# GpSimd's tiles as a subtraction and a max with zero, in halves, in place of eight pointer-scalar minima

## The chip, the cores and the metric

The kernel runs on one core of a Trainium2 chip. A core has TensorE (PE in the profile), VectorE (DVE), ScalarE (ACT), GpSimd (POOL) and SyncE (SP), which here only issues DMAs. Each engine works through its own instruction stream in order; semaphores order the engines against each other. The metric is device time of one launch in microseconds, as the median of several runs. All data are float32.

## The reference, cut to what matters

Four graph layers run over 64 graphs of 256 nodes with 128 features. Each takes `relu(layernorm(x))` and adds its result to x. Layers 0 to 2 are matrix products with a 256 x 256 adjacency and small weights, with gates, and together they make the "front" of the kernel below. Layer 3 is the heavy one: it needs, for every pair of nodes (i, j) of a graph and each of 256 hidden features, one leaky ReLU.

```
def _L3_gnn_ref(x, W, b_lin, a, bias):          # W and bias are the adjacency
    W1, W2 = (W[:, :F], W[:, F:])
    s1 = jnp.einsum('bkf,ef->bke', x, W1)
    s2 = jnp.einsum('bkf,ef->bke', x, W2)
    pre = s1[:, :, None, :] + s2[:, None, :, :] + b_lin
    h = jnp.where(pre >= 0, pre, ALPHA * pre)
    e = jnp.einsum('bije,e->bij', h, a) + bias
    attn = jax.nn.softmax(e, axis=2)
    out = jax.nn.sigmoid(jnp.einsum('bij,bjf->bif', attn, x))
```

A leaky ReLU is ALPHA times its argument plus (1 - ALPHA) times the ReLU. The part linear in s1 drops out of the softmax, the part linear in s2 is one product (`lin`), and what is left is the sum over e of a[e] (1 - ALPHA) relu(s1[i, e] + s2[j, e]).

## The kernel before

Graphs are handled in 32 pairs (NB = 2). For one pair, `front(p)` computes layers 0 to 2 and the operands of layer 3: s1 in two feature halves, `s1a` (features 0 to 127) and `s1b` (128 to 255), each 128 partitions x 2 graphs x 256 nodes, and minus s2 in the same two halves. The first half of minus s2 stays in a PSUM bank (`s2a`) with a copy in SBUF (`s2c`); the second is in SBUF (`s2n`), and ScalarE copies it to a PSUM bank (`s2p`) for itself.

The work of layer 3 is cut into tiles `rl` of 128 features x 4 rows i x 2 graphs x 256 nodes j, that is 128 x 2048 float32. A pair needs 128 tiles: 2 blocks of 128 rows (`ic`), 32 tiles to a block, 2 feature halves. The whole kernel makes 4096. Three engines make them, `work_on_tile(e)`, line 637:

- VectorE makes tiles of the first half alone, each as one minimum of two repeated operands (line 652): min(s1, -s2).
- ScalarE makes tiles of either half with eight activations relu(s1 - (-s2)), 128 x 256 each (line 665). It takes a tile of the first half only where that half lags by two tiles (`half`, line 624).
- GpSimd makes tiles of the second half with eight minima, 128 x 256 each, of `s2n` with a per-partition scalar that is read from a column of `s1b` (line 672). They are made in four parts of two instructions.

min(s1, -s2) is s1 minus relu(s1 + s2), and what is constant over j drops out of the softmax; so a tile of minima serves as well as one of ReLUs, with the weight's sign turned. TensorE sums a tile over the features (`score`, line 696): for each of 4 rows one matmul with a window of weights, `win` for tiles of ReLUs and `win_n` (the negative) for tiles of minima. Two records stand in the trace for each such float32 matmul, so a tile leaves eight.

When a block's 64 tiles are scored, `tail` (line 554) adds the adjacency on VectorE, `lin` on GpSimd (line 562), then softmax and the product with h3, and ends on GpSimd (lines 601 and 602) with the output. GpSimd also takes part in each layernorm (`inverse_root`, lines 258 and 259, and line 331).

The order is not left to the hardware. While the program is built, a planner (lines 751 to 785) plays the schedule with a clock for each engine and a booked cost for each step (`ran`), and `in_order` ties every engine's instructions to the order that came out. What the planner books for tiles is: 2.2 us for a tile of VectorE; 1.43 us (second half, from PSUM) or 1.6 us (first half, from SBUF) for four activations, half a tile; 1.8 us for two minima of GpSimd, a quarter of a tile. Steps of tails go ahead of steps of fronts, and these ahead of tiles; TensorE scores the tile that was done first. There are 13 tile buffers, and an engine holds at most 8 (VectorE), 3 (ScalarE) or 2 (GpSimd) tiles that are being made or wait to be scored. Which engine makes which tile, and when TensorE scores it, is thus fixed by the booked costs; at run time an engine that is later than planned makes TensorE wait at that place in its order. Fronts run about two pairs ahead; a front is spread over 1.7 pairs' worth of scored tiles.

```
    tiles = [[relu_pool.tile([P, 4, NB, N], F32, name=f"rl{k}", bufs=1), 0.0] for k in range(13)]
    MOST = {DVE: 8, ACT: 3, POOL: 2}
```

Of the kernel before, what the change touches and what calls it, by code (L numbers as in the profile page):

```python
# [10 lines left out]
OP = mybir.AluOpType  # L11
# [3 lines left out]
P = 128  # L15
NB = 2
# [4 lines left out]
PE, DVE, ACT, POOL = ENGINES = (mybir.EngineType.PE, mybir.EngineType.DVE, mybir.EngineType.Activation, mybir.EngineType.Pool)  # L21
# [4 lines left out]
def kernel(  # L26
# [19 lines left out]
    a_vec: bass.AP,  # L46
    out: bass.AP,
):

# [25 lines left out]
    nc = tc.nc  # L77
    B, N, D = x.shape
# [19 lines left out]
    def ran(engine, us, *after):  # L98
        start = max(clock[engine], 0.0, *after)
        if engine == ACT:  # L100
            behind[0] = max(0.0, behind[0] - (start - clock[ACT])) + 0.024 * us
        clock[engine] = start + us
        return clock[engine] + SEEN[engine] + (behind[0] if engine == ACT else 0.0)
# [19 lines left out]
    last, done = {}, [0]  # L123
# [112 lines left out]
    win = const.tile([P, NE, 63], F32, name="win")  # L236
    nc.vector.memset(win, 0.0)
    win_n = const.tile([P, NE, 63], F32, name="win_n")
# [27 lines left out]
    def flat(t):  # L266
        return t.rearrange("p b n -> p (b n)")
# [353 lines left out]
    def where(n):  # L621
        return n // SLOTS, n % SLOTS // 32, n % 32

    def half(e):

        return 0 if e == DVE or e == ACT and following[0] <= following[1] - LAG else 1

    def tile_ready(e):

        if e in begun:  # L630
            return 0.0
        n = following[half(e)]
        if n >= NSLOT or n // SLOTS not in READY or held[e] == MOST[e] or not tiles:
            return None
        return max(READY[n // SLOTS]["since"][half(e)], min(t[1] for t in tiles))

    def work_on_tile(e):
        if e not in begun:
            k = half(e)
            tiles.sort(key=lambda t: t[1])  # L640
            begun[e] = [following[k], k, *tiles.pop(0), 0]
            following[k] += 1
            held[e] += 1
        n, k, t, free, part = begun[e]
        p, ic, r = where(n)
        ops = READY[p]
        i0 = ic * P + r
        since = max(ops["since"][k], free)
        if e == DVE:
            whole = [P, 4, NB, N]  # L650
            rows = ops["s1"][0][:, :, i0:i0 + 97:32].rearrange("p b g -> p g b").unsqueeze(3)
            nc.vector.tensor_tensor(t, rows.to_broadcast(whole), ops["s2a"].unsqueeze(1).to_broadcast(whole), op=OP.min)  # L652
            done = ran(DVE, 2.2, since)
            t_s2v[p % 2] = done
            parts = 1
        elif e == ACT:
            if k and "s2p" not in ops:
                ops["s2p"] = s2p
                nc.scalar.copy(s2p, ops["s2n"])
                ran(ACT, COPY, since)  # L660
            parts = 2
            for g in (2 * part, 2 * part + 1):
                for b in range(NB):
                    i = i0 + g * 32
                    nc.scalar.activation(t[:, g, b, :], (s2p if k else ops["s2c"])[:, b, :], AF.Relu,  # L665
                                         bias=ops["s1"][k][:, b, i:i + 1], scale=-1.0)
            done = ran(ACT, 1.43 if k else 1.6, since)
        else:
            parts = 4
            for b in range(NB):  # L670
                i = i0 + part * 32
                nc.gpsimd.tensor_scalar(t[:, part, b, :], ops["s2n"][:, b, :], ops["s1"][1][:, b, i:i + 1], None, op0=OP.min)  # L672
            done = ran(POOL, 1.8, since)
        begun[e][4] += 1
        if part + 1 == parts:
            del begun[e]
            made.append((done, n, k, t, e))
# [18 lines left out]
    def score(tile_):  # L696
        since, n, k, t, e = tile_
        p, ic, r = where(n)
        block = p * NC + ic
        pe = pes[block % 2]  # L700
        first = block not in left
        if first:
            left[block] = 64
        made.remove(tile_)
        left[block] -= 1

        w = win if e == ACT else win_n
        for g in range(4):
            nc.tensor.matmul(pe[g * 32:(g + 1) * 32, :], w[:, k, 31 - r:63 - r], flat(t[:, g]),  # L709
                             start=first, stop=(left[block] == 0), skip_group_check=True)  # L710
        free = ran(PE, PROJECT, since, t_pe.get(block - 2, 0.0))
        tiles.append([t, free])
        held[e] -= 1
        scored[0] += 1
        if left[block] == 0:
            begin((p, ic), tail(p, ic, pe, free, READY[p]["x3"], READY[p]["h3"]))
# [6 lines left out]
    def begin(key, steps):  # L723
        CHAINS[key] = [steps, next(steps), 0]
# [7 lines left out]
    def chain_ready(key, e):  # L732

        engine, since, bank, gate = (*CHAINS[key][1], 0, None)[:4] if len(CHAINS[key][1]) < 4 else CHAINS[key][1]
        if engine != e or bank and not spare or gate and not gate():
            return None
        if not isinstance(key, tuple) and key > 0 and spare:

            due = STEPS_OF_FRONT * (scored[0] / (2 * SLOTS) - (key - 2)) / SPREAD
            if CHAINS[key][2] > due + AHEAD:  # L740
                return None
        return max(since, min(b[1] for b in spare)) if bank else since
# [12 lines left out]
    while scored[0] < 2 * NSLOT or CHAINS:  # L755
        while begun_fronts[0] < NPAIR and begun_fronts[0] < 2 + (scored[0] + 2 * SLOTS - 1) // (2 * SLOTS):
            begin_front()
        e = min(now, key=now.get)
        todo = []
        for key in CHAINS:  # L760
            since = chain_ready(key, e)
# [6 lines left out]
        else:  # L768
            since = tile_ready(e)
# [3 lines left out]
        if ready:  # L773
            _, (rank, *_), what = min(ready, key=lambda x: x[1])
            if rank < 2:
                advance(what)
            elif e == PE:
                score(what)
            else:
                work_on_tile(e)  # L780
            in_order()
            now[e] = max(now[e], clock[e])
        else:
            later = [x[0] for x in todo] + [t for t in now.values() if t > now[e]]
            now[e] = min(later) if later else now[e] + 1.0
# [31 lines left out]
```

## Time and profile before

| | |
|---|---|
| median of 3 runs | 5349.16 us (5348.2 to 5349.51) |
| the profiled execution, its own time | 5354.23 us |
| its span, first to last instruction | 5352.4 us |
| TensorE clock granted | 0.996 |
| tiles by VectorE, ScalarE, GpSimd | 2015, 1415, 666 |
| first minimum of GpSimd starts, last one starts | 140.3 us, 5337.2 us |
| last layernorm step on GpSimd (line 258) | 5122.9 us |

The tile counts come from the groups of instructions: 2015 of line 652; 11320 of line 665 (11056 of the second half and 264 of the first) over eight; 5328 of line 672 over eight. A time in a row "busy" is the union of a group's instructions, so that overlapping ones count once; "mean ns" is the duration of one, and on ScalarE and GpSimd consecutive instructions overlap. All four compute engines are busy for 96 to 98 per cent of the span, so the share of busy time alone does not say which of them sets the pace.

### The profile page before, as it was taken

The page shows a single profiled execution, that of the slowest core. Times are in us where ns is not written, and L with a number is a line of the kernel's source. Part 1 is how long each engine was busy: PE and PEld are TensorE (multiplying, and loading weights), DVE is VectorE, ACT ScalarE, POOL GpSimd, SP SyncE. Part 2 cuts the span into 40 slices and gives each one's busy share as a digit, 9 for nine tenths or more (in the row PEclk, how much of TensorE's full clock was granted, in tenths as well). Part 3 has the DMA queues.
Part 4 walks back from the last instruction along what each step waited for, and adds up shares of the span by engine and source line. Part 5 has one row for each costly group of instructions (what it writes and reads, how often), then busy time and mean ns, then how long its engine had stood idle before and what let it go on. Part 6 is the DMA issues. An engine that isn't in the chain of part 4 may idle for free.

```text
span 5352.4 us, 138977 instructions
## 1 busy us (share of the span) xinstructions
PE 5241.4 (98%) x56085; PEld 1861.5 (35%) x56085; DVE 5221.7 (98%) x4322; ACT 5121.4 (96%) x13465; POOL 5160.9 (96%) x5974
## 2 busy tenths in 40 slices
PE   6999999999999999999999999999999999999998
PEld 2333333333333333333333333333333333333332
DVE  3999999999999999999999999999999999999998
ACT  3999999999999999999999999999999999999999
POOL 0999999999999999999999999999999999999999
PEclk9999999999999999999999999999999999999999
DMA  0000000000000000000000000000000000000000
GB/s 17 5 5 6 6 3 6 6 5 6 5 4 6 5 6 5 3 6 6 5 5 4 4 6 5 6 6 3 6 5 6 6 5 3 6 5 4 4 2 4
DMA packets 38839, 26.99 MB, mean 5 GB/s; under 512 B 3504, under 2 KB 38192, under 8 KB 38192
## 3 DMA queue, kind: packets, MB, share of 16 engines
q1 hardware_dynamic: 35088, 17.05, 1.1%
q8 instruction: 438, 7.18, 0.6%
q14 instruction: 209, 1.71, 0.1%
q10 hardware_dynamic: 3104, 1.05, 0.1%
HBM read 9.70 MB, written 8.39 MB: 3 GB/s over the span
## 4 chain that ended last, share of the span: by engine, by line
PE 49%; DVE 34%; POOL 9%; ACT 5%; issue 4%; DMA 0%; POOLq 0%; SPq 0%; DVEq 0%; ACTq 0%
PE bank L709 32%; DVE rl L652 28%; PE bank L264 15%; POOL rl L672 7%; ACT rl L665 3%; PE bank L292 1%; DVE d L404 1%; DVE stats L324 1%; DVE bank L408 1%; DVE hT L412 1%; DVE rh L385 1%; PE bank L285 1%; POOL sc L562 0%; DVE mv L327 0%; POOL mv L259 0%
## 5 line engine op out<-in xcount | busy, mean ns | idle before, releaser
L672 POOL TENSOR_SCALAR rl<-s2n,s1b 128x256 f32<-128x256 f32 x5328 | 4786.0, 940 | 9.7 <-ACT s1b L539 9.7
L652 DVE TENSOR_TENSOR rl<-s1a,bank 128x2048 f32<-128x2048 f32 x2015 | 4484.6, 2276 | 12.1 <-ACT s1a L548 12.1
L665 ACT ACTIVATE rl<-bank,s1b 128x256 f32<-128x256 f32 x11056 | 4392.2, 839 | 1.3
L709 PE MATMUL bank<-rl,win_n 128*32 128x512 f32 x21448 | 2654.8, 593 | 33.9 <-DVE rl L652 31.9
L709 PE MATMUL bank<-rl,win 128*32 128x512 f32 x11320 | 1487.2, 593 | 0.0
L709 PEld LDWEIGHTS bank<-rl,win_n 128*32 128x32 f32 x21448 | 678.9, 110 | 1496.4 <-issue 1214.0
L709 PEld LDWEIGHTS bank<-rl,win 128*32 128x32 f32 x11320 | 365.9, 110 | 754.4 <-issue 630.2
L264 PE MATMUL bank<-adj_t,h 128*32 128x256 f32 x5120 | 310.0, 381 | 3.8 <-ACT h L423 3.8
L264 PEld LDWEIGHTS bank<-adj_t,h 128*32 128x32 f32 x5120 | 166.6, 110 | 174.3 <-issue 58.6
L335 ACT ACTIVATE h<-x,mv 128x128 f32<-128x128 f32 x384 | 172.1, 634 | 43.3 <-POOL mv L331 42.9
L264 PE MATMUL bank<-hT,u3t 128*32 128x512 f32 x1280 | 169.5, 593 | 0.0
L264 PE MATMUL bank<-mT,w4t 128*32 128x512 f32 x1280 | 169.4, 592 | 0.0
L264 PE MATMUL bank<-mT,w 128*32 128x512 f32 x1280 | 166.8, 593 | 0.5 <-ACT bank L381 0.5
L264 PE MATMUL bank<-mT,w5t 128*32 128x512 f32 x1280 | 166.7, 592 | 0.4 <-DVE rh L385 0.4
L264 PE MATMUL bank<-rh,u5t 128*32 128x512 f32 x1280 | 166.6, 592 | 0.0
L341 ACT COPY mT<-bank 128x512 f32<-128x512 f32 x160 | 133.9, 837 | 33.1 <-PE bank L264 24.6
L396 ACT ACTIVATE bank<-bank,gate_b 128x512 f32<-128x512 f32 x160 | 141.0, 881 | 17.7 <-PE bank L264 17.7
L381 ACT ACTIVATE bank<-bank,gate_b 128x512 f32<-128x512 f32 x160 | 140.0, 875 | 15.6 <-PE bank L264 15.2
L399 ACT ACTIVATE bank<-bank,gate_b 128x512 f32<-128x512 f32 x160 | 136.3, 852 | 12.8 <-PE bank L264 12.8
L423 ACT COPY h<-bank 128x512 f32<-128x512 f32 x128 | 117.3, 916 | 29.6 <-PE bank L292 24.7
L258 POOL TENSOR_SCALAR mv<-mv 128x4 f32<-128x4 f32 x128 | 29.8, 232 | 120.1 <-DVE mv L326 112.5
L404 DVE TENSOR_TENSOR d<-bank,hT 128x512 f32<-128x512 f32 x160 | 108.4, 678 | 37.5 <-ACT bank L399 37.5
(116 smaller groups left out, 3445.0 us busy)
## 6 DMA issues: line engine op xcount, KB each, us to landing
xin<-in_x_dram SPq DMA_DIRECT2D x64, 128.0 KB, 2.3
out_dram<-o SPq DMA_DIRECT2D x64, 128.0 KB, 1.8
w_raw<-in_L_gnn_w_w_dram ACTq DMA_DIRECT2D x3, 128.0 KB, 4.3
th_raw<-in_L_gnn_Theta_dram ACTq DMA_DIRECT2D x1, 320.0 KB, 3.1
adj_n<-in_adj_dram SPq DMA_DIRECT2D x1, 256.0 KB, 4.8
w_raw<-in_L_gnn_u_w_dram ACTq DMA_DIRECT2D x2, 64.0 KB, 3.4
bias<-in_L_gnn_bias_dram ACTq DMA_DIRECT2D x2, 64.0 KB, 3.0
w<-in_L_gnn_weight_dram ACTq DMA_DIRECT2D x1, 64.0 KB, 2.8
```

The source lines that it names most:

```text
L264: nc.tensor.matmul(o[g:g + 32], w[:, g:g + 32], t, start=start, stop=stop, skip_group_check=True)
L335: nc.scalar.activation(h[:, k, :], s[:, k, :], AF.Relu, bias=mv[:, k, 0:1], scale=mv[:, k, 1:2])
L341: nc.scalar.copy(c, by_feature(bank[0]))
L381: nc.scalar.activation(r[0], pr[0], AF.Tanh, bias=br, scale=0.5)
L396: nc.scalar.activation(pr[0], pr[0], AF.Tanh, bias=bz, scale=0.5)
L399: nc.scalar.activation(pv[0], pv[0], AF.Tanh, bias=bh, scale=1.0)
L404: nc.vector.tensor_sub(d, by_feature(pv[0]), hT)
L423: nc.scalar.copy(h, by_token(b[0]))
L652: nc.vector.tensor_tensor(t, rows.to_broadcast(whole), ops["s2a"].unsqueeze(1).to_broadcast(whole), op=OP.min)
L665: nc.scalar.activation(t[:, g, b, :], (s2p if k else ops["s2c"])[:, b, :], AF.Relu, bias=ops["s1"][k][:, b, i:i + 1], scale=-1.0)
L672: nc.gpsimd.tensor_scalar(t[:, part, b, :], ops["s2n"][:, b, :], ops["s1"][1][:, b, i:i + 1], None, op0=OP.min)
L709: nc.tensor.matmul(pe[g * 32:(g + 1) * 32, :], w[:, k, 31 - r:63 - r], flat(t[:, g]), start=first, stop=(left[block] == 0), skip_group_che ...
```

## The change

```diff
         else:
-            parts = 4
-            for b in range(NB):
-                i = i0 + part * 32
-                nc.gpsimd.tensor_scalar(t[:, part, b, :], ops["s2n"][:, b, :], ops["s1"][1][:, b, i:i + 1], None, op0=OP.min)
-            done = ran(POOL, 1.8, since)
+            parts = 2
+            whole = [P, 2, NB, N]
+            i = i0 + part * 64
+            rows = ops["s1"][1][:, :, i:i + 33:32].rearrange("p b g -> p g b").unsqueeze(3)
+            g = t[:, 2 * part:2 * part + 2]
+            nc.gpsimd.tensor_tensor(g, rows.to_broadcast(whole), ops["s2n"].unsqueeze(1).to_broadcast(whole), op=OP.subtract)
+            nc.gpsimd.tensor_scalar(g, g, 0.0, None, op0=OP.max)
+            done = ran(POOL, 2.75, since)
...
-        w = win if e == ACT else win_n
+        w = win_n if e == DVE else win
```

A tile of GpSimd is made in two halves of 128 x 1024. Each half is a subtraction s1 - (-s2) of two repeated operands (a value of `s1b` repeated over 256 nodes, `s2n` repeated over two rows), then a max with the immediate zero, in place. The tile is then one of ReLUs like ScalarE's, so TensorE takes `win` for it. The planner books 2.75 us for a half, 5.5 us for a tile where it booked 7.2 us. As the booked cost changes, the planner's order of all engines is made anew.

## The prediction

> **What bounds the kernel now.** I read the busy shares first, then the period of a pair, then the waits inside the steady stretch, then single instructions, then the end.
>
> The steady stretch is read from SP's order of time: a pair's input load is issued once per pair.
>
> ```profile
> 478.79 1.07 SPq L146 DMA_DIRECT2D xin<-in_x_dram  x2
> ...
> 4733.87 0.89 SPq L146 DMA_DIRECT2D xin<-in_x_dram  x2
> ```
>
> Twenty-six pairs lie between these two, so a pair takes 4255.1 / 26 = 163.7 us. Busy time in that stretch, all engines, and then VectorE's tiles alone:
>
> ```profile
> 494.00:4734.00 4240.00, 4211.18 (x45376) 1501.03 (x45368) 4223.99 (x3470) 4129.96 (x10868) 4199.15 (x4855) 1.00 0.02 5
> ...
> 494.00:4734.00 4240.00, 3635.88 (x1634) 1.00 0.02 5
> ```
>
> The columns are PE, PEld, DVE, ACT, POOL. VectorE is idle for 16 of 4240 us, GpSimd for 41, ScalarE for 110. VectorE makes 1634 tiles in 25.9 pairs, 63 per pair. PE's 29 idle us are too few, since its ends are modelled; its real slack shows in its waits (300 to 4900 us):
>
> ```profile
> PEld bank L292 <- DVE hT L412: 63.8, 54, 2.3
> PEld bank L709 <- DVE rl L652: 58.9, 170, 2.0
> PEld bank L709 <- POOL rl L672: 42.7, 138, 1.2
> ...
> DVE nmx L566 <- POOL sc L562: 8.1, 16, 1.0
> ```
>
> A weight load's normal wait is 0.30 us. POOL's 138 waits are nearly all of that kind (138 x 0.3 = 41 of 42.7); VectorE's on hT average 1.2. TensorE waits for VectorE, and VectorE for almost nobody (8.1 us for GpSimd's `sc`): in real time VectorE's queue sets the pair.
>
> In the plan it is TensorE. A tile costs it 0.86 us booked (groups of 8, 16 and 24 records in the order of time take 1.04, 1.90 and 2.76 us, 0.86 apart). Adding the booked steps of `front` and two tails gives 51.9, so a pair is 128 x 0.86 + 51.9 = 162.0 us. VectorE books 63 x 2.2 + 23.4 = 162.0 as well. The real pair is 1.7 us longer since VectorE's small steps run longer than booked. This matters: the plan cannot get shorter than 162 by a faster GpSimd, and VectorE keeps its 63 tiles.
>
> GpSimd, VectorE and ScalarE in order of time:
>
> ```profile
> 2184.14 12.59 POOL L672 TENSOR_SCALAR rl<-s2n,s1b 128x256 f32<-128x256 f32 x14
> 2196.68 1.32 POOL L562 TENSOR_TENSOR sc<-sc,lin 128x512 f32<-128x512 f32 x1
> 2197.94 14.38 POOL L672 TENSOR_SCALAR rl<-s2n,s1b 128x256 f32<-128x256 f32 x16
> 2212.41 0.41 POOL L601 TENSOR_SCALAR o<-o 128x256 f32<-128x256 f32 x1
> 2212.90 0.74 POOL L602 TENSOR_TENSOR o<-o,x 128x256 f32<-128x256 f32 x1
> 2213.61 26.93 POOL L672 TENSOR_SCALAR rl<-s2n,s1b 128x256 f32<-128x256 f32 x30
> ...
> 2198.63 8.87 DVE L652 TENSOR_TENSOR rl<-s1a,bank 128x2048 f32<-128x2048 f32 x4
> 2207.42 0.16 DVE L592 RECIPROCAL rs<-sums 128x2 f32<-128x2 f32 x1
> ...
> 2193.06 3.53 ACT L665 ACTIVATE rl<-bank,s1b 128x256 f32<-128x256 f32 x8
> 2195.91 1.15 ACT L519 COPY s2c<-bank 128x512 f32<-128x512 f32 x1
> ```
>
> From start to start a pointer minimum takes 12.54 / 14 = 0.896 us, so two are 1.79 (booked 1.8) and a tile 7.17; VectorE's tile takes 8.79 / 4 = 2.20 (booked 2.2); four activations 2.85 / 2 = 1.43 (booked 1.43). The add over 512 takes 1.26, over 256 0.71, the immediate tensor_scalar over 256 0.49 to the next, which reads its result.
>
> The end:
>
> ```profile
> 5080.00:5130.00 50.00, 46.25 (x512) 17.21 (x504) 49.69 (x48) 50.00 (x139) 49.34 (x60) 1.00 0.01 2
> 5230.00:5280.00 50.00, 43.61 (x379) 11.17 (x372) 50.00 (x25) 50.00 (x143) 50.00 (x56) 1.00 0.00 1
> ```
>
> The last front leaves GpSimd at 5123 us. From about 5030 on TensorE has less to do, and in the last 220 us all three makers are full while TensorE waits. There, and only there, a faster maker is worth time directly.
>
> **What the Trainium skill says.** "GPSIMD Engine Reference", section 3.1, gives 4497 ns for an add over 2048 float32 and calls about 2.6 cycles an element at 1.2 GHz the rate of two-input work, and 1.03 cycles the port's limit for short bodies. The trace agrees with the first: (1.26 - 0.71) / 256 = 2.15 ns, 2.58 cycles. "SBUF — State Buffer", section "Who interferes with whom", says that a VectorE instruction with at most one SBUF input does not contend with GpSimd. Line 652 reads one operand from PSUM, and the 64 adds of line 562 lie within 1260 to 1377 ns; I count no contention. "Perfetto Trace Analysis", section "GPSIMD Engine Instruction", advises start-to-start spacing over reported spans; I follow it (0.896 against a mean span of 0.940).
>
> **The change part by part.** Removed: eight minima per tile, 7.17 us. Added per half: one subtraction and one max over 1024, with a dependence between them. No row shows an operation with repeated operands on GpSimd.
>
> Upper estimate from rows: subtraction 0.71 + 768 x 2.15 ns = 2.36. The max: a 128x4 tensor_scalar takes 0.23 and one of 256 0.41, so 0.70 ns an element and 0.95 over 1024. The gap before a dependent instruction is 0.08 (2212.82 to 2212.90). Sum 3.4, a tile 6.8 us. Max as such is not dear: line 258 runs as add and as max, with medians of 232 and 233 ns (over only four elements).
>
> Lower estimate: two reads at the page's 1.03 cycles are 1.72 ns an element; 0.16 fixed + 1.76 + 0.81 for the max without its start = 2.73. So a half is 2.7 to 3.4 us, and the plan books 2.75.
>
> I take 2.75. The booked tile figures above (1.8, 2.2, 1.43) equal the trace's spacing within 1 per cent, whereas GpSimd's small steps are booked too low (1.05 against 1.26 for line 562), so the figure deserves weight but not certainty. It also equals the port estimate. The rows I extrapolate are all in place and without repeated operands.
>
> How many tiles would the planner give GpSimd? TensorE binds the plan, VectorE makes 63, so GpSimd and ScalarE share 65 per 162 us, 0.401 per us, under their limits of held tiles. With a wait W before scoring, 2 / (5.5 + 0.86 + W) + 3 / (2.86 + 0.86 + W) = 0.401 gives W = 7.8: GpSimd 23, ScalarE 42 (before: 21 and 44). Without the limit GpSimd would make (162 - 11) / 5.5 = 27.
>
> Steady stretch: GpSimd's real pair is 23 x 5.5 + 13.5 = 140 of 163.7 (13.5 is before's rest: 163.7 - 20.9 x 7.17). VectorE still sets 163.7. ScalarE loses two tiles of 2.86: hidden behind VectorE. Gain 0 to 9 us, namely VectorE's wait for `sc`; I take 3. The tail steps on GpSimd may stand behind a half of 2.75 instead of two minima of 1.8; this is in the plan and costs nothing while VectorE is full.
>
> End: over 300 us GpSimd makes 300 / 5.5 - 300 / 7.17 = 12.7 tiles more, at a joint rate of 0.99 per us (1/2.2 + 1/2.86 + 1/5.5) worth 12.8 us; part of this stretch is still bound by TensorE, so 12.
>
> No DMA, load or semaphore between engines is moved except through the plan. The weights (`win`) cost the same: matmuls with win and with win_n both take 593 ns.
>
> Sum: span 5352.4 - 15 = 5337. The profiled execution took 5354.2 in all; the median of runs, 5349.2, lies 3.2 below its span: 5334 us.
>
> **Rivals.**
>
> R1, half a us short. A half of 2.9 to 3.26: the steady stretch holds (23 x 6.52 + 13.5 = 163.5), but at the end GpSimd's share, made for 5.5, runs late: 52 tiles x (c - 5.5) for a tile of c us. At c = 6.0 that is +26 - 15 = +11, at 6.5 +37: 5345 to 5390.
>
> R2, slower: GpSimd becomes the bound. From 3.26 us a half (6.53 a tile) 23 tiles and 13.5 exceed 163.7; TensorE, bound to its order, waits at every tile of GpSimd. At 3.4: 23 x 6.8 + 13.5 = 169.9, +6.2 over 30 pairs = 187, and 52 x 1.3 = 68 less 3 at the end: about +250, 5600 us. With 25 tiles per pair it would be 5990, with 22 about 5400. For it: every two-input row of GpSimd, and the page's. Against: the booked tile figures.
>
> R3, the slack is worth more. With ScalarE and GpSimd less pressed, VectorE's small steps come at better moments and the pair falls to the plan's 162.0: 1.7 x 30 = 50 us more, 5285. Against it: VectorE has just 16 us of idleness in 4240 to give back.
>
> **How the numbers follow.** Forecast 0.50, R1 0.13, R2 0.33, R3 0.04. The forecast's own range is 5318 to 5346 (end gain 3 to 20, steady 0 to 9). The low end, 5320, leaves out R3; the high end, 5600, cuts off half of R2. About 0.2% (10.7 us) is what can be told from no change. Faster: 0.39 of the forecast, R3, a little of R1, 0.45; same 0.13; slower: R2, most of R1, 0.42.
>
> **What would show it.** The rows of the two new instructions decide: subtraction near 1.9 and max near 0.85 start to start for the forecast, 2.4 and 1.0 for R2. The count of halves, about 1470 (23 x 32 tiles, two each), shows the share. Under the forecast the pair stays at 163.7 with VectorE full and GpSimd idle for some 20 us of it; under R2 VectorE and ScalarE show idleness, PE waits on POOL rl, GpSimd is full. It would be wrong if VectorE's 63 tiles per pair changed.

## The result and the profile after

The changed kernel takes 7968.7 us (median of 4 runs, 7967.4 to 7969.7) where the kernel before takes 5349.0 (also 4 runs): a ratio of 1.490, 95% interval 1.487 to 1.492. It is slower by half, far outside the predicted range.

Groups of instructions of the changed kernel, the two new lines first: count, then busy us and mean ns of one, then the engine's idle time before them and what ended it.

```profile
L676 POOL TENSOR_SCALAR rl<-rl 128x1024 f32<-128x1024 f32 x1568 | 4336.8, 2766 | 137.3
L675 POOL TENSOR_TENSOR rl<-s1b,s2n 128x1024 f32<-128x1024 f32 x1568 | 2982.5, 1902 | 9.6 <-ACT s1b L540 9.6
L653 DVE TENSOR_TENSOR rl<-s1a,bank 128x2048 f32<-128x2048 f32 x2008 | 4497.9, 2280 | 760.1 <-PE bank L713 735.5
```

The subtraction takes 1.90 us, about what was forecast. The max behind it takes 2.77 us; it was put at 0.95 at most. There are 1568 halves, 784 tiles or 24.5 per pair. VectorE, which waited for almost nothing before, is now idle for 760 us in front of its tiles alone.

GpSimd in order of time:

```profile
3009.41 1.91 POOL L675 TENSOR_TENSOR rl<-s1b,s2n 128x1024 f32<-128x1024 f32 x1
3011.41 2.76 POOL L676 TENSOR_SCALAR rl<-rl 128x1024 f32<-128x1024 f32 x1
3014.14 1.90 POOL L675 TENSOR_TENSOR rl<-s1b,s2n 128x1024 f32<-128x1024 f32 x1
3016.12 2.77 POOL L676 TENSOR_SCALAR rl<-rl 128x1024 f32<-128x1024 f32 x1
```

From start to start the subtraction takes 1.99 us and the max 2.73, so a half is 4.72 and a tile 9.44 us, where eight pointer minima took 7.17 and the plan books 5.5. Apart from some 0.09 us before each max, which reads what the subtraction wrote, GpSimd works here without a gap.

The chain of waits of the changed kernel, as shares of the span by engine (before it was PE 49%, DVE 34%, POOL 9%):

```profile
POOL 79%; PE 8%; DVE 6%; ACT 4%; issue 2%; POOLq 0%; DMA 0%; SPq 0%; ACTq 0%; DVEq 0%
```

The input loads on SP's queue, one per pair, in order of time:

```profile
661.26 0.90 SPq L147 DMA_DIRECT2D xin<-in_x_dram  x2
...
7017.97 0.90 SPq L147 DMA_DIRECT2D xin<-in_x_dram  x2
```

In 26 pairs 6356.7 us pass, 244.5 a pair. GpSimd's own sum is 24.5 x 9.44 + 13.5 (its small steps, as in the prediction) = 244.8. So GpSimd alone sets the pair. The pair is 80.8 us longer than before. Of the 2616 us by which the spans differ, 2102 lie in these 26 pairs, 182 ahead of them and 331 behind. As an estimate, thirty such pairs are 2424, and the end, where the prediction's 52 tiles are booked at 5.5 and take 9.44, is 205 more: 2629. How the others stand behind it, from the waits between 300 and 7000 us (total us, times, longest):

```profile
PEld bank L713 <- POOL rl L676: 891.8, 375, 4.6
ACT h L336 <- POOL mv L332: 796.6, 108, 20.7
...
DVE nmx L567 <- POOL sc L563: 655.5, 54, 15.4
DVE rl L653 <- PE bank L713: 599.0, 246, 6.0
```

TensorE waits at GpSimd's tiles in its fixed order; VectorE waits for TensorE to free a tile buffer; and the steps of layernorm and softmax that pass through GpSimd are late for all.

### The profile page after: what moved, and what is told of

Same layout as the page of the kernel before. It is cut to its first block, busy times and chain, and to the rows that moved or that the text cites. A ratio compares the mean times of both kernels' runs of the same rounds, so it can differ in the third digit from the quotient of the medians.

```text
span 7967.9 us, 135700 instructions
## 1 busy us (share of the span) xinstructions
PE 6086.3 (76%) x56085; PEld 1994.5 (25%) x56085; DVE 5279.4 (66%) x4315; ACT 4846.7 (61%) x12577; POOL 7642.8 (96%) x3782
## 4 chain that ended last, share of the span: by engine, by line
POOL 79%; PE 8%; DVE 6%; ACT 4%; issue 2%; POOLq 0%; DMA 0%; SPq 0%; ACTq 0%; DVEq 0%
POOL rl L676 45%; POOL rl L675 29%; PE bank L713 4%; DVE rl L653 4%; PE bank L265 3%; ACT rl L666 2%; POOL mv L260 2%; POOL sc L563 1%; POOL o L603 1%; DVE stats L325 1%; ACT h L336 1%; POOL rn L260 0%; DVE hT L413 0%; DVE mv L328 0%; POOL o L602 0%
## 5 line engine op out<-in xcount | busy, mean ns | idle before, releaser
L676 POOL TENSOR_SCALAR rl<-rl 128x1024 f32<-128x1024 f32 x1568 | 4336.8, 2766 | 137.3
L666 ACT ACTIVATE rl<-bank,s1b 128x256 f32<-128x256 f32 x10112 | 3870.0, 569 | 97.2 <-PE bank L713 95.4
L713 PE MATMUL bank<-rl,win 128*32 128x512 f32 x16704 | 2957.4, 646 | 789.2 <-POOL rl L676 788.5
L675 POOL TENSOR_TENSOR rl<-s1b,s2n 128x1024 f32<-128x1024 f32 x1568 | 2982.5, 1902 | 9.6 <-ACT s1b L540 9.6
L713 PE MATMUL bank<-rl,win_n 128*32 128x512 f32 x16064 | 2754.7, 641 | 3.1 <-DVE rl L653 3.1
L713 PEld LDWEIGHTS bank<-rl,win 128*32 128x32 f32 x16704 | 656.2, 116 | 2216.3 <-POOL rl L676 1157.9
L386 DVE SCALAR_TENSOR_TENSOR rh<-bank,hT 128x512 f32<-128x512 f32 x160 | 110.0, 688 | 607.3 <-ACT bank L382 607.3
L397 ACT ACTIVATE bank<-bank,gate_b 128x512 f32<-128x512 f32 x160 | 110.8, 692 | 522.2 <-PE bank L265 522.2
L265 PE MATMUL bank<-adj_ti,h 128*32 128x256 f32 x1024 | 111.9, 613 | 305.8 <-ACT h L336 305.8
L265 PE MATMUL bank<-mT,w 128*32 128x512 f32 x1280 | 283.1, 705 | 0.5 <-ACT bank L382 0.5
L265 PEld LDWEIGHTS bank<-adj_t,h 128*32 128x32 f32 x5120 | 169.7, 112 | 189.1 <-issue 86.7
```

The lines of the kernel that those rows point to most:

```text
L265: nc.tensor.matmul(o[g:g + 32], w[:, g:g + 32], t, start=start, stop=stop, skip_group_check=True)
L386: nc.vector.scalar_tensor_tensor(rh, by_feature(r[0]), 1.0, hT, op0=OP.add, op1=OP.mult)
L397: nc.scalar.activation(pr[0], pr[0], AF.Tanh, bias=bz, scale=0.5)
L675: nc.gpsimd.tensor_tensor(g, rows.to_broadcast(whole), ops["s2n"].unsqueeze(1).to_broadcast(whole), op=OP.subtract)
L676: nc.gpsimd.tensor_scalar(g, g, 0.0, None, op0=OP.max)
```

## Experiments

A ratio below is always against the kernel before, run beside it on the same chip (its medians were 5347.3 to 5358.6 us). Three questions were open: why the second pass is slow, how much of the loss is the slow instruction and how much its false booking, and whether the rest of the prediction (VectorE sets the pair, a faster GpSimd changes nothing in it) would have held with a fast second pass.

### GpSimd's operations alone

A kernel of nothing but GpSimd instructions, each form eight times; these are the forms that are used below, by their lines. `rows` and `reps` are repeated operands as in the change; `a`, `z` are contiguous 128x1024; `v` is 128x256.

```
101  tensor_tensor(rows, reps, subtract)       110  tensor_scalar(a, 1.0, mult)
104  tensor_tensor(a, z, add)                  111  tensor_scalar(a, 0.5, 0.5, mult, add)
106  tensor_scalar(a, 0.0, max)                112  tensor_scalar(a, 0.0, is_gt)
107  the same, in place                        114  tensor_scalar(v, 0.0, max)
109  tensor_scalar(a, 0.0, add)                116  tensor_scalar(v, pointer, min)
                                               117  tensor_scalar(v, pointer, subtract)
```

> The layers are left out: the output is constants, and GpSimd alone runs 8 instructions of each of 23 forms, for their start-to-start spacing. Theory A (the operation is dear: min and max on GpSimd's tensor_scalar cost about 2.6 ns an element whatever else): max and min with an immediate over 1024 near 2.73 us in place or not, add and mult over 1024 near 0.9; over 256 max near 0.75, add near 0.37, and min with a pointer near 0.9 while subtract with a pointer is near 0.5. Theory B (the form is dear: in place behind the subtraction, or a long 128x1024 pattern): max not in place near 0.9, and mult or add over 1024 as dear as max. Theory C (it runs slow only beside busy engines): max near 0.9 here. Subtraction of repeated operands near 1.9 to 2.0, add of contiguous ones 2.36 if in-place or plain operands are what made the rows of before dearer.

In order of time (start, us for all eight):

```profile
23.36 14.90 POOL L101 TENSOR_TENSOR o<-s,n 128x1024 f32<-128x1024 f32 x8 [22.94 <-DVEq L152]
...
67.94 18.41 POOL L104 TENSOR_TENSOR o<-big,zero 128x1024 f32<-128x1024 f32 x8
...
114.91 21.87 POOL L106 TENSOR_SCALAR o<-big 128x1024 f32<-128x1024 f32 x8
136.75 21.87 POOL L107 TENSOR_SCALAR o<-o 128x1024 f32<-128x1024 f32 x8
...
180.42 21.91 POOL L109 TENSOR_SCALAR o<-big 128x1024 f32<-128x1024 f32 x8
...
224.17 8.10 POOL L111 TENSOR_SCALAR o<-big 128x1024 f32<-128x1024 f32 x8
```

None of the three theories held. Max takes 2.73 us alone, so neighbours are not to blame (C falls); in place or not is the same, and so cannot be the reason; but add and mult with one immediate take 2.73 too (A falls). What is fast is the one form with two immediates, mult then add: 1.01 us, over the same long pattern (so the pattern is not the reason either, and B falls). It is the form of line 601, GpSimd's only immediate tensor_scalar over more than four elements in the trace before. With a pointer over 256, min and subtract take 0.89 and 0.90, so the minima of the kernel before are slow in the same way, not because they are minima.

The subtraction of repeated operands takes 14.86 / 8 = 1.86 us against 2.30 for an add of contiguous operands, which also is 2.30 in place. Over 2048 elements it takes 3.58, so 1.68 ns for each element more.

### The plan's booking, apart from the slow pass

Two kernels take one half of the change each. The first books truly what the changed kernel does:

```diff
-            done = ran(POOL, 2.75, since)
+            done = ran(POOL, 4.72, since)
```

> The changed kernel with 4.72 us booked for a half instead of 2.75. Theory A1 (most of the loss is the false booking, which gave GpSimd 24.5 tiles per pair that it cannot make in time): makers' booked balance is 0.910 T = 150 tiles, T = 165 us against 162, so about 5352 x (165 + 1.7) / 163.7 = 5450 us, and GpSimd about 16 tiles per pair. Theory A2 (the slow instructions disturb others whatever the plan says): over 5600 us.

5604.6 us, a ratio of 1.046 (1.044 to 1.048). The second keeps the minima of before and books them as short as the change does:

```diff
-            done = ran(POOL, 1.8, since)
+            done = ran(POOL, 1.375, since)
```

> The kernel before, its minima booked at 1.375 us for two instead of 1.8, that is 5.5 us a tile as in the change. Theory A1: the plan gives 24 to 25 tiles per pair, 24.5 x 7.17 + 13.5 = 189 us a pair, about 30 x 25.5 above before plus the end: 6150 to 6250 us. If the booking matters little: 5350 us.

6189.4 us (one run), 189.1 us a pair, as expected: a false booking alone costs 16 per cent without one slower GpSimd instruction. The true booking took back 2364 of the 2620 us, but did not come down to the 5450 expected. Its tiles:

```profile
L666 ACT ACTIVATE rl<-bank,s1b 128x256 f32<-128x256 f32 x12128 | 4849.2, 974 | 1.1
L653 DVE TENSOR_TENSOR rl<-s1a,bank 128x2048 f32<-128x2048 f32 x2048 | 4552.9, 2278 | 67.5 <-ACT s1a L549 67.5
...
L675 POOL TENSOR_TENSOR rl<-s1b,s2n 128x1024 f32<-128x1024 f32 x1064 | 2024.8, 1903 | 9.6 <-ACT s1b L540 9.6
```

VectorE makes all 2048 tiles of the first half, 64 a pair, and ScalarE none of them. The expectation had pooled the three makers; but VectorE cannot make tiles of the second half, so ScalarE and GpSimd have to make its 64 a pair between them. GpSimd's 16.6 tiles are 16.6 x 9.44 + 13.5 = 170 us, and the pair takes 170.6 (4434.5 / 26). The kernel does not wait for GpSimd alone there: TensorE waits longest for VectorE, and VectorE, ScalarE and GpSimd are idle for only 84, 83 and 118 of 4420 us between 500 and 4920. Which of them sets this pair was not separated.

### The second pass as other operations

First a single multiplication in place of the max (the theory of a dear max):

```diff
-            nc.gpsimd.tensor_scalar(g, g, 0.0, None, op0=OP.max)
+            nc.gpsimd.tensor_scalar(g, g, 1.0, None, op0=OP.mult)
```

> The changed kernel with a multiplication by one in place of the max with zero: the ReLU of GpSimd's tiles is left out. Theory A: the second pass takes about 0.9 us, a half 2.9, a tile 5.8; 24.5 x 5.8 + 13.5 = 156 is under 163.7, VectorE sets the pair, the end gains nothing or a little: 5335 to 5375 us, which is what the prediction said for this cost. Theory B: the second pass stays near 2.7 us and the time near 7970 us.

7978.9 us, 1.489 (1.487 to 1.491), the second pass at 2.77 us as before. Then the fast form of the list:

```diff
-            nc.gpsimd.tensor_scalar(g, g, 0.0, None, op0=OP.max)
+            nc.gpsimd.tensor_scalar(g, g, 1.0, 0.0, op0=OP.mult, op1=OP.add)
```

> The changed kernel, 2.75 us booked, with the second pass as mult by one plus zero in one tensor_scalar: the ReLU of GpSimd's tiles is left out. If the form of the second pass is the whole loss, a half takes 1.99 + 1.0 = 2.99, a tile 5.97; 24.5 x 5.97 + 13.5 = 160 is under 163.7, so VectorE still sets the pair, and the end runs 52 x 0.47 = 24 us late less 15 gained: 5350 to 5390 us. If something else of the change costs as well (the subtraction beside busy engines, the reordered plan): over 5450 us.

5416.0 us, 1.013 (1.011 to 1.015). One more operation in the same instruction takes away 2553 us of the changed kernel's time. Its second pass:

```profile
L676 POOL TENSOR_SCALAR rl<-rl 128x1024 f32<-128x1024 f32 x1568 | 1639.8, 1046 | 137.4
```

Still 26 us above what was expected. A half takes 2.99 where 2.75 are booked, so GpSimd runs late against the plan though its sum, 160, is under the pair. The pair is 165.1 us, and VectorE waits 45.5 us for GpSimd's `sc` between 300 and 5000 us, where it was 8.1 before. Over the 28 or so pairs that is 1.3 us each, most of what the pair is longer by.

### Which pairs of operations are fast

> The layers are left out again: GpSimd alone, 8 instructions of each of 21 two-operation tensor_scalar forms. In the first list mult by 0.5 with add of 0.5 took 1.01 us over 1024 where every single operation took 2.73. Theory D1 (any second operation takes the fast path): mult+max, max+add and the like all near 1.0. Theory D2 (mult then add alone is a path of its own): mult+add near 1.0, all others, add+mult too, at 2.73 or above, since two operations do more work than one. With a pointer over 256 (one operation 0.90): mult by a pointer then add near 0.4 if the pointer does not matter, near 0.9 or more if it does.

> The layers are left out: GpSimd alone, 8 instructions of each of 15 forms. In the list before, min 9 with max 0 took 1.1 us over 1024 where max alone took 2.73. If the pair min, max is a fast path: near 1.01 in place or not and with 3e38; max then min and add then max stay near 3.6. The question for the kernel before is a minimum with a pointer and an idle max with -3e38 over 256: near 0.46 if the fast path takes pointers as mult with add did (0.457), near 1.1 if not (0.894 for the plain pointer minimum).

Of the first of these two lists: 101 is mult+add, 102 mult+max, 109 add+mult, 111 min 9 + max 0.

```profile
23.36 8.11 POOL L101 TENSOR_SCALAR o<-big 128x1024 f32<-128x1024 f32 x8 [22.94 <-DVEq L150]
31.44 28.77 POOL L102 TENSOR_SCALAR o<-big 128x1024 f32<-128x1024 f32 x8
...
211.87 8.11 POOL L109 TENSOR_SCALAR o<-big 128x1024 f32<-128x1024 f32 x8
...
248.84 8.87 POOL L111 TENSOR_SCALAR o<-big 128x1024 f32<-128x1024 f32 x8
```

Neither D1 nor D2: mult+add, mult+mult, add+mult and min+max take 1.0 to 1.1 us; every other pair of immediates tried (mult+max, max+mult, max+add, add+max, max+max, max+min, add+add, mult+subtract, mult+min) takes 3.6 to 3.7, more than one operation. What sets the four apart, beyond their operations and the order of these, no run here shows. The second list has the pair that matters for the kernel before: 107 is min with a pointer and max with -3e38 over 128x256, 115 the plain pointer minimum.

```profile
111.71 3.61 POOL L107 TENSOR_SCALAR o<-n,s 128x256 f32<-128x256 f32 x8
...
146.72 7.19 POOL L115 TENSOR_SCALAR o<-n,s 128x256 f32<-128x256 f32 x8
```

An idle second operation halves it, 0.448 against 0.894 us.

### The change as it was meant

min with 3e38 and max with zero is the max alone in value, and it is a fast pair:

```diff
-            nc.gpsimd.tensor_scalar(g, g, 0.0, None, op0=OP.max)
-            done = ran(POOL, 2.75, since)
+            nc.gpsimd.tensor_scalar(g, g, 3.0e38, 0.0, op0=OP.min, op1=OP.max)
+            done = ran(POOL, 3.0, since)
```

> The changed kernel with its max written as min with 3e38 and max with zero in one tensor_scalar, the value is the same, and 3.0 us booked for a half. If the clamp runs as in the list, 1.01 us, a half takes 2.99 as booked. Then the rest of the prediction is put to the test: GpSimd in time, 163.7 us a pair set by VectorE, the end shorter by some 9 us: 5330 to 5350 us. If the second pass is slow in the kernel all the same, near 8000; if GpSimd's longer grains delay its small steps even when they are booked right, as in the run before where the pair took 165.1 us: 5370 to 5400 us.

5351.8 us, a ratio of 1.0007 (0.9998 to 1.0015): no change. The group of its subtractions:

```profile
L675 POOL TENSOR_TENSOR rl<-s1b,s2n 128x1024 f32<-128x1024 f32 x1472 | 2801.2, 1903 | 130.2 <-PE bank L713 119.8
```

Its input loads, 26 pairs apart:

```profile
481.31 0.89 SPq L147 DMA_DIRECT2D xin<-in_x_dram  x2
...
4738.89 0.90 SPq L147 DMA_DIRECT2D xin<-in_x_dram  x2
```

And busy time (PE, PEld, DVE, ACT, POOL) in most of the stretch between them:

```profile
480.00:4670.00 4190.00, 4172.71 (x44908) 1482.47 (x44904) 4181.86 (x3439) 3923.63 (x10306) 3725.18 (x2867) 1.00 0.02 5
```

1472 halves are 23.0 tiles a pair. The pair takes 163.75 us, VectorE is idle for 8 of 4190 us, GpSimd for 465 (it was 41 of 4240). So the steady stretch behaves as the prediction said: GpSimd's gain turns into GpSimd's idleness, since VectorE sets the pair. The end's 9 us do not show in the total. Between the profiles, what lies behind the last of these loads is 7.4 us shorter than before (611.1 for 618.5), while the loads come 2.5 to 5.0 us later; but the profiled execution of before was itself 5 us above its median, so two profiles do not settle so small a gain.

### What would use the room

Four further kernels change the minima of before, or the booking of VectorE's tile, or both.

```diff
-  nc.gpsimd.tensor_scalar(t[:, part, b, :], ops["s2n"][:, b, :], ops["s1"][1][:, b, i:i + 1], None, op0=OP.min)
-  done = ran(POOL, 1.8, since)
+  nc.gpsimd.tensor_scalar(t[:, part, b, :], ops["s2n"][:, b, :], ops["s1"][1][:, b, i:i + 1], -3.0e38, op0=OP.min, op1=OP.max)
+  done = ran(POOL, 0.9, since)
```

> The kernel before with a second operation, max with -3e38, on GpSimd's pointer minima (the value is the same), 0.9 us booked for two. In the list such a minimum took 0.448 instead of 0.894 us, so a tile 3.6 instead of 7.2. Under the reading that VectorE's 63 tiles set the pair and the plan cannot get under TensorE's 162.0: no gain in the steady stretch, 163.7 a pair, a few us at the end: 5325 to 5350 us, GpSimd 25 tiles a pair and idle for a third of it. If GpSimd's speed counted as such: clearly under 5300.

With the next line changed as well:

```diff
-            done = ran(DVE, 2.2, since)
+            done = ran(DVE, 2.26, since)
```

> The same, and VectorE's tile booked at 2.26 instead of 2.2 us, so that its share in the plan falls to (162 - 23.4) / 2.26 = 61.3 tiles, which with its real rest of 25.2 takes 160 us. TensorE, at about 161 to 162, or ScalarE, then sets the pair: about 162, 5290 to 5310 us. If VectorE was not what set the pair, 5325 to 5350 as in the run without it.

That line alone in the kernel before:

> The kernel before with VectorE's tile booked at 2.26 alone. ScalarE has to take the 1.7 tiles a pair that VectorE gives up, and with 44 + 1.7 tiles at 2.86 and a rest of some 35 us it needs 166: 5370 to 5430 us, slower, so that the booking pays only where GpSimd has made room. If ScalarE has that room already: 5290 to 5310.

And that line in the change with the clamp, booked at 3.0:

> The change with the clamp, 3.0 us booked for a half, and VectorE's tile booked at 2.26. GpSimd makes 23 tiles a pair (151 us), VectorE 61.3 (160), ScalarE 43.7 (160): about 162 a pair, 5290 to 5320 us. If nothing but the tail can be won: 5340 to 5352.

| kernel | us | ratio to before (95%) | us a pair | VectorE's tiles |
|---|---|---|---|---|
| clamped pointer minima | 5276.8 | 0.987 (0.986 to 0.988) | 162.2 | 1999 |
| the same, VectorE booked at 2.26 | 5268.9 | 0.985 (0.984 to 0.987) | 161.9 | 1947 |
| before, VectorE booked at 2.26 | 5381.7 | 1.007 (1.005 to 1.008) | 164.3 | 1983 |
| change with clamp, VectorE at 2.26 | 5312.7 | 0.994 (0.992 to 0.995) | 162.5 | 1959 |

The tiles are those of the whole kernel. The first row beats both kernels without a word about VectorE, which I had not expected. Busy time of that kernel, of all engines and of VectorE's tiles alone:

```profile
480.00:4670.00 4190.00, 4189.15 (x45272) 1491.93 (x45264) 4185.57 (x3458) 3705.18 (x9583) 2827.99 (x6097) 1.00 0.02 5
...
480.00:4670.00 4190.00, 3627.97 (x1629) 1.00 0.02 5
```

VectorE is full, and GpSimd idle for a third. In all VectorE makes 16 tiles fewer than before, but not in this stretch: 1629 in 25.8 pairs are 63 a pair, as before. What fell is the rest of its time. Its idleness went from 0.6 to 0.2 us a pair (16 of 4240, then 4 of 4190), and its busy time from 163.0 to 162.0. Over half of that one microsecond is one small step of layernorm, which runs four times a pair, before and here:

```profile
L327 DVE TENSOR_SCALAR mv<-mv 128x4 f32<-128x4 f32 x128 | 47.1, 368 | 4.4
...
L327 DVE TENSOR_SCALAR mv<-mv 128x4 f32<-128x4 f32 x128 | 27.2, 212 | 4.4
```

It waits for GpSimd, as the traces read: in the change with the clamp 34 of the 128 take longer than 0.6 us, in the last row of the table 68, and every one of them ends 0.02 to 0.03 us after an instruction of GpSimd ends (in the kernel before 7 of 9). With less idleness and shorter steps the pair falls by 1.5 us, to 162.2. Between the two profiles 38 of the 76 us lie in the 26 pairs and 35 behind the last of their loads, at the end, where I had allowed a few us.

The second row, with VectorE booked longer, is the fastest kernel found, below the 5290 that was expected at least; TensorE, whose ends are modelled, shows no idle time there in 4190 us. The last row moves the change by 39 us against the same kernel with VectorE at 2.2 (5351.8), and the two differ in that booking alone and in the plan that follows from it: with 61.2 tiles a pair for VectorE the pair is 162.5 us.

The third row is the control: the booking alone loses, as expected. Its load at 506 us is out of step with the others, so its pair is read from the next one on:

```profile
647.40 1.84 SPq L146 DMA_DIRECT2D xin<-in_x_dram  x2
...
4755.69 0.89 SPq L146 DMA_DIRECT2D xin<-in_x_dram  x2
```

In 25 pairs 4108.3 us pass, 164.3 a pair, where the kernel before takes 163.6 over the same 25. That makes some 18 of the 27.5 us between the profiles. The expectation had 166; VectorE gave up one tile a pair and not 1.7. VectorE is idle for 75 of 4090 us there; fewer tiles for it paid only in the kernels where GpSimd had room. Which wait sets this pair was not separated.

## Why the prediction was wrong

**What bounds the kernel before**: right for the change that was asked about. That VectorE's queue sets 163.7 us a pair, and that a GpSimd tile of 5.98 us gains nothing in the steady stretch, is shown by the change with the clamp (163.75 us, GpSimd with time to spare), and from the other side by the same kernel with fewer VectorE tiles (162.5). That no faster GpSimd could gain there is not so: with tiles of 3.6 us the pair came down to 162.2 with VectorE's 63 tiles. That is what rival R3 described, VectorE's small steps and waits getting shorter until the pair is the plan's 162.0; it had been given a chance of 0.04 for this change, and with the clamped change the pair stayed at 163.75.

**No contention**: right for VectorE's tiles (2.20 us from start to start before, with the clamp, and with the clamped minima), but not for all of VectorE. The step of line 327 takes 0.37 us in the mean before and 0.17 at its shortest, so waiting for GpSimd costs it at most 0.8 us a pair. The page cited there (the Trainium skill, "SBUF — State Buffer", section "Who interferes with whom") makes an exception for VectorE's 2-port modes, which the prediction left out; whether line 327 runs in one no trace here shows.

**The subtraction**: right at its lower estimate, 1.9 us; it measured 1.86 alone and 1.99 with the gap before the max. The upper estimate, 2.36 from contiguous rows at 2.15 ns an element, fell: with repeated operands the whole instruction takes 1.82 ns an element. The lower estimate's 1.72 ns for two reads is close to the 1.68 measured for each further element; that the reads are the reason is not shown.

**The max**: the step that failed. The prediction says: "The max: a 128x4 tensor_scalar takes 0.23 and one of 256 0.41, so 0.70 ns an element and 0.95 over 1024." The row of 256, line 601, is mult then add, a fast pair, and the row of 4, line 258, is a single operation: the slope was drawn through two kinds of instruction. A single operation takes 2.73 us over 1024, nearly three times the 0.95. Both ends of the range for a half, 2.7 to 3.4, shared this term, so 4.72 was outside it. The remark that max runs like add on line 258 was true and no help, as both are slow; over four elements nothing of it shows. What the profile did hold was the warning: a pointer minimum over 256 took 0.90 us, more than twice line 601 over the same size. I laid that on the operation that was removed and did not ask whether the new one was of its kind.

**The choice of 2.75 for the forecast**: the booked figure was taken because the other tile figures agree with the trace. It was wrong by 1.97 us. What another line of the plan books says nothing on an instruction that this kernel had not run.

**Who bounds after**: the rival R2, "GpSimd becomes the bound", was right in mechanism, with the waits it named, and mis-sized. Its sum with the measured half and its own 23 tiles is 230.6 us; the planner gave 24.5, which makes 244.8 against 244.5 measured. The count was the smaller error. (23.0 came out where 3.0 was booked.) Two small sums of the prediction are off: R2's 5990 us for 25 tiles is some 20 short by the sum that gave 5600, and the forecast's lower end, 5318, should be 5320.

**The end**: the forecast's 12 us are not shown; with the clamp, where it should have been 9, the total did not differ from before. That a faster maker is worth time there is borne out by the clamped pointer minima: by the prediction's own sum for the last 300 us a tile of 3.6 us would be worth about 38 (an estimate: 41 tiles more at a joint rate of 1.08 per us), and between the profiles the end is 35 us shorter. The steady stretch gave as much again, though not directly: through VectorE's small steps.

Put together, most of the loss needs both parts of the change, the slow pass and its false booking; each alone costs less:

| booked for a half | second pass 2.73 us | second pass 1.0 us |
|---|---|---|
| 2.75 | 1.490 | 1.013 |
| as measured (4.72; 3.0) | 1.046 | 1.0007 |

The lower right kernel keeps the ReLU through the clamp; the upper right one leaves it out.

## What to carry to other kernels

Take an instruction's price from a row with the same number and kind of operations, not only the same engine, size and opcode name; if two rows of the same size differ by a factor of two, find out what separates them before extrapolating from either. In a schedule laid down from booked costs, a cost booked too low on one engine is a wait on all of them: here it cost 16 per cent with no instruction changed. And a faster maker that does not set the pace pays little in the steady stretch: nothing at 6.0 us a tile, and 1.5 of 163.7 us at half the cost of before, through steps of the engine that does. It pays where all makers are full, as at the end, and where the plan takes work from the engine that sets the pace.

## What the runs showed of the hardware

- GpSimd's tensor_scalar over 128x1024 float32 takes 2.73 us with one operation (max, min, add, mult and is_gt alike), 1.0 to 1.1 us with mult+add, mult+mult, add+mult or min+max, in this order, and 3.6 to 3.7 us with the other pairs tried. With one pointer over 128x256 it is 0.89 to 0.90 with one operation, 0.45 to 0.46 in a fast pair, and 1.11 to 1.12 in a slow one.
- GpSimd's tensor_tensor over 1024 takes 1.86 us with both operands repeated and 2.30 with contiguous ones; add, subtract and mult of repeated operands cost the same.
- VectorE's tensor_scalar over 128x4 float32 (line 327, or 328 in the changed kernels) takes 0.17 us at its shortest and up to 1.9 beside a busy GpSimd. With the clamp in the change, all that took over 0.6 us (34 of 128, and 68 of 128 with VectorE booked at 2.26) ended 0.02 to 0.03 us after a GpSimd instruction ended.
- The granted TensorE clock fell to 0.879 in the changed kernel, where TensorE often waits (0.996 before, and 0.996 again with the clamp); its 512-column matmuls took 641 to 646 ns instead of 593. GpSimd's own sum gives the pair's time without it; why the clock fell was not tested.
